# Moving the splitting of the turned x on VectorE, with other buffers for two x tiles and other steps for the weight splits, in a retention and feed-forward kernel

## The chip, the cores and the metric

The kernel runs on one core of one Trainium2 chip. The metric is the time of one execution on the device in microseconds (us), lower being better; the time of a kernel is the median of several runs. A profile is one execution taken by the hardware profiler: its span runs from the first instruction to the last. TensorE (matmul) is called PE in the profile, its weight loads PEld, VectorE is DVE, ScalarE is ACT, GpSimd is POOL and SyncE is SP; SP issues nearly all transfers of this kernel, in order.

## The reference

The input is `x`, four sequences of 1024 tokens with 512 features, in fp32. Two blocks follow each other, each wrapped by a layer norm before it, a layer norm after it and a residual addition.

```python
x = x + layernorm(attn(layernorm(x)))
x = x + layernorm(ffn(layernorm(x)))

def attn(x):                       # 16 heads of 32 features
    q, v = x @ Wq.T, x @ Wv.T
    ret = scan(v)                  # state = lam * state + v, along the tokens
    out = layernorm(q * ret) * gamma + beta
    return (out * silu(x @ Wg.T)) @ Wo.T

def ffn(x):                        # 512 -> 1536 -> 512, weights rounded to fp8
    gate = silu(x @ gate_w * gate_scale)
    return ((gate * (x @ up_w * up_scale)) @ down_w) * down_scale
```

## The kernel before

**Rounds and steps.** The 4096 tokens are worked on in eight blocks of 512 tokens (`TB`), each of four tiles of 128 tokens (`s` = 0 to 3). The features lie in four chunks of 128 (`c`). The main loop (`for t in range(NB)`, line 1221) has eight rounds; each has twelve steps `i`, one for each 128 of the 1536 inner features. In round `t` three blocks are in work. `f` is the feed-forward part of block `t`: in each step PE runs `f.gate(i)` (tile `pfg`), `f.up(i)` (`pfu`) and, two steps later, `f.down` (`pd`). `b` is the retention part of block `t + 1`, whose matmuls are put between those of the feed-forward part. `n` is block `t + 2`, whose x is loaded, normed and turned so that it can be used from step 11 on. `l` is the feed-forward part of the block before, which is finished in the first steps of the round.

**Order.** Every instruction of an engine runs in the order in which the program issues it (`InOrder`, line 66). So the position of a call in the long loop body is its place in the queues of all engines that it uses, and an instruction that waits holds back everything behind it on its engine. Buffers are tiles with a tag; a tag has a fixed number of slots that are handed out in turn, and a new tile waits until the last user of its slot is done.

**Three ways to project.** Blocks 0 and 1 use plain fp32 matmuls. Blocks 2 and 3 (`fast`) use a scheme with seven products of half size for each of the projections v, q and g. Blocks 4 to 7 (`by_parts`, `PARTS` = 4) use three passes for each chunk. For these the turned x and the weights are each split into a top part (a mask on the bits, `TOP_MASK`), the rest (`low`) and a combination (`diff`). `begin` runs the pass with the top part of the weights and the turned x, then the pass with `low`; `end` runs the pass with `diff`. The first `begin` (`v`, chunk 0) is issued in step 11 of the round before, right behind `f.up(11)` (`n.gap(-2)`). A pass multiplies by all 512 tokens, so it needs all four quarters of its operand. The output projection of every block from 2 on uses the seven products (`product`, tile `po`): in steps 7, 8 and 9, three, three and one of them. The first two are copied by ACT and the other five added by VectorE (`add_o`, tile `mids`); the order of the products is 1, 2, 6, 5, 3, 7, 4, and two PSUM banks are shared among them, so that a product which goes on in a bank waits until the addition of the one before has read it. Operands of the products are `y`, which VectorE finishes in step 6 (`gate_y`), and sums of its parts (`y_sums`).

**The turned x.** For block `t + 2`, in rounds 1 to 5, ACT norms x tile 0 in step 6, tiles 1 and 2 in step 7 and tile 3 in step 8 (`norm_x`, tile `xn`). VectorE turns each by blocks into a second tile, and SP sends it to DRAM (`send_x`, transfer `mx<-xn`). SP fetches it back in another layout (`fetch_x`, transfer `xnT<-mx`). For blocks 4 to 7, VectorE then makes for each quarter the mask and the rest (`low_of`: `top`, then `low`) and the combination (`diff_of`). For blocks 3 to 7 the normed and the turned tile are the halves of one pair, with a tag of a single slot (`xn`).

**The x1 tiles.** When the output products are added, `o_moments` takes means and variances on VectorE, POOL forms the power -1/2, ACT scales (`x1_of`) and POOL adds the residual x. `x1_moments` then takes the moments of this sum on VectorE, and `x1n_of` norms it. Tiles 0 and 1 go through this in steps 8 and 9, tiles 2 and 3 in steps 9, 10 and 11.

**The weight splits.** The weights of v, q and g are split for the three passes in twelve units (`Splitter`), during rounds 1 and 2. A unit is loaded by two transfers, split by three VectorE instructions and one POOL instruction (`split`, behind the step's `fuse`), and stored by two transfers at the end of the step (`store`). They are needed from the end of round 2 on. The condition `splits` says in which steps a unit is worked on.

## Time and profile before

| what | us |
|---|---|
| median of 3 runs (lowest, highest) | 985.81 (984.67, 986.65) |
| the profiled execution's own time | 983.96 |
| its span | 982.1 |
| PE busy | 952.0 (97%) |
| DVE busy | 682.5 (69%) |
| ACT busy | 427.5 (44%) |
| POOL busy | 279.5 (28%) |

The granted clock of TensorE is 0.995 of full speed over the span. The median of the runs lies 1.85 us above the profiled execution. Busy time is the time in which an engine executes an instruction; idle time before an instruction is put down to what released it. In the timelines below, a row holds the start, the duration, the engine, the instruction with its output and inputs, and in brackets the idle time before it with what ended it.

### The profile page before, as it was taken

The numbers are of one execution on the slowest core, as the hardware profiler recorded it, in microseconds if no ns is written. First come the engines' busy times: TensorE is split into PE (matmuls) and PEld (weight loads), VectorE is DVE, ScalarE is ACT, GpSimd is POOL, SyncE is SP. The second block draws the span as 40 slices with busy tenths as digits, with TensorE's granted clock in tenths as the row PEclk, the third lists the DMA queues.
The fourth block names the chain that finished last, engine by engine and source line by source line (L and its number), as shares of the span: only waits on it lengthen the run. The fifth ranks groups of instructions, "written<-read, shape, count | busy, mean of one in ns | idle before, by whom it ended". The sixth has DMA issues, their size and how long they took to land.

```text
span 982.1 us, 11944 instructions
## 1 busy us (share of the span) xinstructions
PE 952.0 (97%) x4022; PEld 746.3 (76%) x4022; DVE 682.5 (69%) x1054; ACT 427.5 (44%) x673; POOL 279.5 (28%) x340
## 2 busy tenths in 40 slices
PE   9999999999989999999999999999999999999996
PEld 7456766677868887778878788778878788788885
DVE  5996998768777877685476845867457765647445
ACT  3556674467645216332263424434263342624223
POOL 1405122403426134240242505322052322314020
PEclk9999999999999999999999999999999999999999
DMA  9311424766648556356454564555453564414021
GB/s 311 107 64 56 138 65 108 238 214 204 225 149 249 179 162 217 106 168 195 149 184 137 145 201 138 163 161 184 149 176 124 156 208 140 142 63 129 1 86 43
DMA packets 115500, 148.14 MB, mean 151 GB/s; under 512 B 10864, under 2 KB 60016, under 8 KB 115440
## 3 DMA queue, kind: packets, MB, share of 16 engines
q1 hardware_dynamic: 114576, 146.73, 47.7%
q8 instruction: 32, 0.52, 0.2%
q10 hardware_dynamic: 864, 0.66, 0.2%
q14 instruction: 28, 0.23, 0.1%
HBM read 108.02 MB, written 42.47 MB: 153 GB/s over the span
## 4 chain that ended last, share of the span: by engine, by line
PE 60%; DVE 17%; DMA 6%; ACT 6%; POOL 5%; issue 4%; SPq 1%; DVEq 0%; ACTq 0%; POOLq 0%
PE pfu L74 11%; PE pfg L74 10%; PE pd L74 9%; PE pv L74 9%; PE pq L74 8%; PE pg L74 6%; PE po L74 5%; DVE st L74 3%; DVE y L74 2%; DMA mx<-xn 1%; DVE gate L74 1%; SPq L74 1%; DVE mids L74 1%; DVE xs L74 1%; POOL mv L74 1%
## 5 line engine op out<-in xcount | busy, mean ns | idle before, releaser
L74 PE MATMUL pfu<-x1nT,up_sb 128*128 128x512 f32 x768 | 200.0, 402 | 1.8 <-DVE gate L74 1.8
L74 PE MATMUL pfg<-x1nT,gate_sb 128*128 128x512 f32 x768 | 194.8, 395 | 0.1
L74 PE MATMUL pd<-down_sb,fuse 128*128 128x512 f32 x720 | 184.1, 397 | 0.0
L74 PEld LDWEIGHTS pfu<-x1nT,up_sb 128*128 128x128 f32 x768 | 143.9, 188 | 36.2 <-DVE gate L74 3.9
L74 PEld LDWEIGHTS pfg<-x1nT,gate_sb 128*128 128x128 f32 x768 | 144.0, 188 | 30.4 <-DVE x1nT L74 0.9
L74 PEld LDWEIGHTS pd<-down_sb,fuse 128*128 128x128 f32 x720 | 135.5, 188 | 28.0
L74 ACT CAST fuse<-gate 128x512 fp32r<-128x512 f32 x90 | 55.7, 619 | 173.8 <-DVE gate L74 173.7
L74 DVE SCALAR_TENSOR_TENSOR gate<-pfu,us_sb,gate 128x512 f32<-128x512 f32 x96 | 71.7, 747 | 57.1 <-PE pfu L74 53.8
L74 ACT ACTIVATE gate<-pfg,gs_sb 128x512 f32<-128x512 f32 x96 | 65.6, 683 | 99.1 <-PE pfg L74 99.1
L74 POOL TENSOR_SCALAR mv<-mv 128x1 f32<-128x1 f32 (+1 forms) x82 | 24.7, 301 | 261.1 <-DVE mv L74 258.1
L74 DVE TENSOR_TENSOR fuse<-gate,fuse 128x512 fp32r<-128x512 f32 x90 | 76.6, 851 | 5.5 <-ACT fuse L74 5.5
L74 DVE BATCH_NORM_STATS2 st<-x 128x6 f32<-128x512 f32 x64 | 43.6, 681 | 20.7 <-POOL x L74 18.2
L74 POOL TENSOR_TENSOR ysum<-y 128x512 f32<-128x512 f32 (+1 forms) x10 | 12.0, 1201 | 148.2 <-DVE y L74 148.1
L74 POOL TENSOR_TENSOR mv<-mv,nhalf 128x1 f32<-128x1 f32 (+1 forms) x75 | 52.0, 694 | 6.2
L74 POOL TENSOR_TENSOR x<-x,x1n 128x512 f32<-128x512 f32 x32 | 45.7, 1432 | 10.0 <-ACT x1n L74 9.2
L74 POOL TENSOR_TENSOR d<-d,x 128x512 f32<-128x512 f32 x28 | 36.5, 1324 | 16.2 <-ACT d L74 10.8
L74 POOL TENSOR_TENSOR sqsum<-sqsum,sq 128x512 f32<-128x512 f32 x24 | 35.0, 1457 | 15.2 <-ACT sq L74 13.7
L74 POOL TENSOR_TENSOR ysum<-ysum,y 128x512 f32<-128x512 f32 (+1 forms) x20 | 24.1, 1203 | 53.5 <-DVE y L74 53.2
L74 DVE TENSOR_TENSOR y<-pq,y 128x512 f32<-128x512 f32 x18 | 12.4, 691 | 35.3 <-PE pq L74 35.3
L74 DVE RECIPROCAL rstd<-rstd 128x512 f32<-128x512 f32 x8 | 26.8, 3352 | 11.9 <-ACT rstd L74 11.9
L74 ACT ACTIVATE xn<-x,mv 128x512 f32<-128x512 f32 x28 | 22.2, 811 | 25.2 <-DMA mx<-xn 24.9
L74 PE MATMUL po<-w_ring_parts,t_sums 128*128 128x256 f32 x128 | 30.4, 380 | 2.3 <-issue 2.3
(199 smaller groups left out, 1616.4 us busy)
## 6 DMA issues: line engine op xcount, KB each, us to landing
kept<-x SPq DMA_DIRECT2D x32, 256.0 KB, 2.1
x<-kept SPq DMA_DIRECT2D x32, 256.0 KB, 4.4
x<-in_x SPq DMA_DIRECT2D x28, 256.0 KB, 3.9
w_ring_parts<-dsum_o SPq DMA_DIRECT2D x28, 256.0 KB, 2.7
out<-d SPq DMA_DIRECT2D x27, 256.0 KB, 2.0
mx<-xn SPq DMA_DIRECT2D x20, 256.0 KB, 2.0
xnT<-mx SPq DMA_DIRECT2D x64, 64.0 KB, 2.2
w_ring_parts<-dtop_v SPq DMA_DIRECT2D x16, 256.0 KB, 3.2
```

The costliest lines, as they stand in the source:

```text
L74: return lambda *args, **kwargs: tc.keep_in_program_order(op(*args, **kwargs))
```

## The change

Four things change, all for the later blocks.

- In `norm_x` and `send_x`, tiles 0 and 2 of blocks 3 to 7 take two slots of the tag `tok` (four slots, also used for the feed-forward outputs `d`, the `late` tiles and the normed x1 tiles) for the normed and the turned x. Tiles 1 and 3 keep the pair.
- `low_of(0)` moves from the end of step 7 into step 8, behind that step's first output product and ahead of `f.up(8)`. `low_of(1)` and `low_of(2)` move from the end of step 8 into step 9, behind the last output product and ahead of `x1_moments` of tiles 0 and 1.
- `low_of(3)` moves from ahead of `f.up(10)` to behind the `x1_moments` of tiles 2 and 3 in step 10; `x1n_of(2)` now stands ahead of `diff_of(3)`.
- The units of the weight splits are worked on in steps 1, 3, 4, 5, 8 and 9 of round 1 (before: 1 to 6, 8 and 9) and in steps 0 to 5 of round 2 (before: 0 to 3).

```diff
@@ norm_x
-            if self.t < 3:
+            if self.t < 3 or s % 2 == 0:
                 xn = work.tile([P, D], F32, tag="tok", name=f"xn_{self.t}_{s}", bufs=4)
@@ send_x
             if self.t < 3:
                 sq = work.tile([P, D], F32, tag="ret", name=f"xs_{self.t}_{s}")
+            elif s % 2 == 0:
+                sq = work.tile([P, D], F32, tag="tok", name=f"xs_{self.t}_{s}", bufs=4)
             else:
                 sq = self.pair[:, 1, :]
@@ main loop
-            splits = (t == 1 and 1 <= i < 10 and i != 7) or (t == 2 and i < 4)
+            splits = (t == 1 and i in (1, 3, 4, 5, 8, 9)) or (t == 2 and i < 6)
...
             if fast and 7 <= i < 10:
                 b.product()
+            if n and n.by_parts and i in (8, 9):
+                for s in ([0], [1, 2])[i - 8]:
+                    n.low_of(s)
...
-            if n and n.by_parts and i == 10:
-                n.low_of(3)
             if fast and i == 10:
                 b.x1_of(2)
                 b.x1_of(3)
...
             if fast and i == 10:
                 b.x1_moments(2)
                 b.x1_moments(3)
                 if n and n.by_parts:
+                    n.low_of(3)
+                b.x1n_of(2)
+                if n and n.by_parts:
                     n.diff_of(3)
-                b.x1n_of(2)
...
-            if n and n.by_parts and i in (7, 8):
-                for s in ([0], [1, 2])[i - 7]:
-                    n.low_of(s)
```

## The prediction

> **What bounds the kernel now.** I read the page's busy shares, then TensorE's waits, then its timeline, and last the timelines of the engines that it waits for.

> ```profile
> PE 952.0 (97%) x4022; PEld 746.3 (76%) x4022; DVE 682.5 (69%) x1054; ACT 427.5 (44%) x673; POOL 279.5 (28%) x340
> ```

> TensorE is busy for 97% of the span. None of its work changes, so only its gaps, 30 us in all, can move. The waits say where they lie (total, times, longest):

> ```profile
> PE po L74 <- issue: 9.3, 4, 3.6
> PE pfu L74 <- DVE gate L74: 1.8, 5, 0.6
> PE po L74 <- DVE mids L74: 1.7, 3, 0.7
> ```

> The largest gaps stand at the output products (`po`, steps 7 to 9 of a round) and at step 11's `pfu`. Below I write `t/i` for round t, step i, and count from the start of step 7's `pfg` in its round: 273.21 (t=1), 398.59, 518.00, 633.17, 748.83 and 865.25 (t=6). Round 6 prepares no later x and has no gap there: it gives the undisturbed clock. In it `po` 1 starts at 1.81, `pfu` 7 at 3.35, the seventh product at 23.13 and the next `pfu` at 24.67. The others take 30.21, 30.24, 25.99, 26.46 and 27.18 us from `pfg` 7 to that `pfu`: 5.54, 5.57, 1.32, 1.79 and 2.51 lost in t=1 to 5. TensorE's timeline (start, duration, instructions, idle time before them and what ended it) has the two large gaps, the seventh product to the low pass in t=3, and the seventh product of t=6:

> ```profile
> 278.80 3.65 PE L74 MATMUL po<-w_ring,y 128*128 128x256 f32 x8 [3.62 <-issue]
> ...
> 418.35 3.51 PE L74 MATMUL po<-w_ring,t_sums 128*128 128x256 f32 x8 [3.38 <-issue]
> ...
> 542.34 1.99 PE L74 MATMUL po<-w_ring_parts,y 128*128 128x256 f32 x8 [0.73 <-DVE mids L74]
> ...
> 555.54 2.11 PE L74 MATMUL pfu<-x1nT,up_sb 128*128 128x512 f32 x8 [0.31 <-DVE gate L74]
> ...
> 558.43 1.07 PE L74 MATMUL pv<-low,w_ring_parts 128*128 128x512 f32 x4
> 559.34 1.99 PE L74 MATMUL pd<-down_sb,fuse 128*128 128x512 f32 x8
> ...
> 888.38 1.89 PE L74 MATMUL po<-w_ring_parts,y 128*128 128x256 f32 x8
> ```

> After a gap of 3.4 us eight `po` matmuls take 3.5 to 3.65 us; undisturbed they take 1.89. The table by stretches names the cause (stretch, length, busy time of PE, PEld, DVE, ACT and POOL, then the granted clock, DMA share and GB/s):

> ```profile
> 275.20:278.80 3.60, 0.00 (x1) 0.03 (x1) 3.53 (x7) 2.52 (x3) 1.32 (x3) 0.98 0.27 80
> 278.80:282.10 3.30, 3.30 (x9) 2.35 (x9) 3.23 (x4) 0.95 (x3) 2.07 (x2) 0.50 0.00 0
> ...
> 766.50:768.10 1.60, 1.59 (x8) 1.42 (x9) 0.57 (x1) 1.00 (x2) 0.00 (x0) 1.00 1.01 338
> ```

> It is 0.50 after 3.6 us of idleness, and still 1.00 after the 1.49 us gap of t=5.

> VectorE's timeline in t=3 shows what the change touches:

> ```profile
> 526.93 0.43 DVE L74 TENSOR_SCALAR top<-xnT 128x512 int32<-128x512 int32 x1 [2.55 <-DMA xnT<-mx]
> ...
> 531.68 0.71 DVE L74 STREAM_TRANSPOSE xn<-xn 128x512 f32<-128x512 f32 x1 [2.97 <-ACT xn L74]
> ...
> 544.38 0.69 DVE L74 TENSOR_TENSOR mids<-po,mids 128x512 f32<-128x512 f32 x1 [1.01 <-PE po L74]
> ...
> 554.74 0.74 DVE L74 SCALAR_TENSOR_TENSOR gate<-pfu,us_sb,gate 128x512 f32<-128x512 f32 x1
> 556.00 0.69 DVE L74 BATCH_NORM_STATS2 st<-x 128x6 f32<-128x512 f32 x1 [0.52 <-POOL x L74]
> ...
> 557.36 0.69 DVE L74 BATCH_NORM_STATS2 st<-x 128x6 f32<-128x512 f32 x1 [0.44 <-POOL x L74]
> ```

> Early in the stage VectorE stands still, with the products' additions queued behind it (526.93, 531.68); over all rounds its waits and ACT's say:

> ```profile
> DVE top L74 <- DMA xnT<-mx: 14.9, 4, 5.1
> ...
> ACT xn L74 <- DMA mx<-xn: 24.9, 5, 7.2
> ```

>  From the seventh product's addition (544.38) on it has almost no pause, and the next gaps of TensorE wait for it.

> **The change, part by part.**

> *Token buffers (t=1 to 5).* `norm_x(2)` no longer waits until `send_x(1)`'s transfer has left the pair; ACT waits there 24.9 us in five rounds, and VectorE's transposition waits for ACT (2.97 above). Nothing is added. The token slots are used 12 times a round instead of 8. The slot of `d` is stored by 500.9 in t=3 and taken at 517.9, and `late`'s stores in t=2 are issued by 394.0 and the slot taken at 400.0, so I cost the extra turns at 0. Without that cover the price is one store, 2.0 us from issue to landing.

> *`low_of(0)` from 7 to 8, behind the fourth product.* It is 0.43 and 0.69 us of work; its wait for the transfer (14.9 us in four rounds) goes, since the data arrive 8.9 to 12.4 us after `pfg` 7 and it now comes at about 15.1. With both waits gone VectorE adds products 3, 4 and 6 when TensorE ends them (10.9, 14.4, 21.5); the next uses of those banks are at 19.6, 16.0 and 23.1. So steps 7 to 9 run as in round 6 and the 1.32, 1.79 and 2.51 us come back in t=3 to 5. No DMA is moved on SP except the two sends, which come earlier.

> *`low_of(1)`, `low_of(2)` and `low_of(3)`: where it is paid.* The first two take 2.13 us (539.47 to 541.60). They lay ahead of the sixth product's addition; they now come after the seventh's, which cannot start before 25.06 (round 6: 890.31). All that follows on VectorE moves back by 2.13: moments, `diff_of`, `x1n_of`, and the moments of output tiles 2 and 3. From the latter a chain through POOL's power, ACT's scaling and POOL's addition leads to the moments of x1: 4.51 us from 551.49 to 556.00 and 6.76 to the end of the second (558.25); round 6 gives 4.36 and 6.73 with less on VectorE, so this chain is latency and does not shrink. `low_of(3)`, formerly ahead of `fuse` 10, now waits for its end, and the low pass of step 11 waits for `low_of(3)`, needing all four quarters. Counted from the seventh addition: second moments end at 13.87 (558.25 - 544.38) + 2.13 = 16.00, `low_of(3)` at 17.14, low pass at about 17.2, with 0.1 for restarting. It was at 14.05 (558.43 - 544.38). So the low pass starts at 25.06 + 17.2 = 42.27, the `pd` behind it at 43.28. On the way `pfu` 11 waits about 1.5 us for `fuse` 10, and the low pass some 1.9; undisturbed they would start at 35.75 and 38.51. That `pd` now starts at 41.34, 41.82 and 42.56 in t=3 to 5. Cost: 1.94 + 1.46 + 0.72 = **+4.12**, gains of the previous paragraph included. Behind it, `x1n_of(2)`, `diff_of(3)`, `fuse` 11 and `x1n_of(3)` keep their distance from `pd` within 0.1.

> The price of `low_of` beside POOL is not shown there. Bounds: 0.43 + 0.69 alone, or, from the split instructions beside POOL's sums (358.00 to 360.60), 1.10 for the second, 0.8 us more a round. I take the low value: by the distances above POOL's additions end at 25.5 and the first mask starts at 25.7. The other bound, below, is VectorE's work without the POOL latency: 0.52 + 1.07 + 0.44 = 2.0 us less a round. That ACT/POOL chain is equal in round 6, so I don't take it.

> *Splits.* One is 1.78 us of VectorE (265.01 to 266.79) and 1.05 of POOL, with two loads and two stores on SP. In 1/6 it stood ahead of `gate_y(0)` and `gate_y(1)`, whose results product 1 needs. Without it `gate_y(0)` ends at 3.70 after `pfg` 7 and `gate_y(1)` at 4.40; the six matmuls that need the second take 1.16, so `pfu` 7 starts at 5.65 instead of 8.89: **-3.24**, half of it clock. In 1/2, the split delayed the addition at 236.04, which waits for a product ended by 234.8, and with it POOL's row sum and `mu` (waits of 0.20 and 0.65): about 1.0 of the step's 11.41 us, between 0.5 and 1.3: **-1.0**. In 2/4 it costs nothing: 1/4 has it and takes the same 11.21 us as 2/4 without. In 2/5 it puts t=2 where t=1 is without 1/6: `pfu` 7 is 2.3 late. Its `pd` after the low pass then starts at 43.28 + 2.3 = 45.58, and was at 45.59: **0**. On SP the issues of a split (0.3 to 0.6 us each) go ahead of the loads of x in 2/4, issued by 385.4 and first used at 393.0, and of the last weights for step 7, issued at 395.1; on POOL its 1.05 goes ahead of the additions of `d` and of a power that 2/6 needs at 397.0. The slack of 5 us and more covers them; without it each would cost its own 2 us.

> Sum: -3.24 - 1.0 + 0 + 4.12 = **-0.1 us**. The profiled execution took 983.96 (its span 982.1 and 1.9 around it), 1.85 below the median of the runs, 985.81; against the median the forecast is 985.7.

> [...] The trace: 3.38 us of idleness brought the clock down, 1.49 did not. [...] A DVE `TENSOR_SCALAR` of x1n takes 0.54 alone (319.02) and 1.50 beside POOL's `t_sums` (320.29). [...]

> **The rivals.** *Slower, by the clock.* The gaps at the low pass (1.9 after 1.5, with 2.9 us of work between) and at product 1 in t=1 and 2 (1.8 and 0.7) may also halve the clock. At 418.35 the halved clock cost 1.75 us beyond the gap (product and `pd` took 5.31 to 423.66, undisturbed 3.56), at 278.80 1.2 (six matmuls took 2.3, not 1.16). Six places of about 1.5 give up to +9, two of them already +3: 989 to 995. It decides from the second place. For it: gaps crowd in steps 10 and 11. Against: 1.49 at 766.51 and 1.16 plus 0.46 at 195 to 196 left 1.00.

> *Faster, by a shorter moments chain.* If the x1 moments in step 10 did not wait for POOL, each of four low passes would come up to 2.0 earlier: -2 to -8, 978 to 984. The equal 4.36 to 4.51 in all rounds speaks against it.

> *The masks' waits stay.* If the sends or turned x still arrive late, t=3 to 5 keep their losses and pay 3.2 a round in addition: about +5, 991. Data arriving 3 us before use in the slowest round speak against it.

> **How the numbers follow.** My forecast, within a few steps' errors of nothing (1.7 us): 0.58, of which 0.46 is within 0.2% (2 us, about what a measurement here can tell from no change), 0.06 faster, 0.06 slower. Clock 0.20, shorter chain 0.14, waits that stay 0.08. So faster 0.20, same 0.46, slower 0.34. The range leaves out the far halves of the faster and slower cases: 982 to 991.

> **What would show it.** Right: no gap above 0.3 us at `po` 3 to 7; `DVE top <- DMA` and `ACT xn <- DMA` gone; a new wait of the `pv` low pass for VectorE's `low`, near 1.9 us in four rounds; `pfu` 11 waiting 1.5; `po` 1 waiting 1.8 in t=1 and t=2; clock 1.00 throughout. Wrong: low passes at 40 after `pfg` 7, or PEclk of 0.5 in step 11.

## The result, and the profile after

| | before | after |
|---|---|---|
| median, us | 985.3 | 992.39 |
| lowest and highest of six runs | 984.34, 987.34 | 989.44, 995.48 |
| profiled execution, its span | 983.96, 982.1 | 991.58, 989.8 |
| mean granted clock in it | 0.995 | 0.992 |

The runs of this table were made beside each other. The ratio after to before is 1.007, with a 95% interval of 1.0048 to 1.0091: the change makes the kernel slower, by 0.7%. The forecast was "no change", 985.7, and its range ended at 991; it was wrong, and the rival "Slower, by the clock" (989 to 995) came true.

The busy shares hardly move. PE's 2.3 us more are the first hint, since it executes the same 4022 matmuls:

```profile
PE 954.3 (96%) x4022; PEld 748.0 (76%) x4022; DVE 679.1 (69%) x1054; ACT 427.3 (43%) x673; POOL 273.0 (28%) x340
```

TensorE's waits after (total, times, longest) have changed places. The gaps of the products by `issue` fell from 9.3 to 3.7 us in all and are at most 1.8 long. The wait of the low pass for VectorE's `low` is new, 8.6 us in four rounds, and `pfu` 11 waits three times as long as before:

```profile
PE pv L74 <- DVE low L74: 8.6, 4, 2.4
PE pfu L74 <- DVE gate L74: 5.5, 5, 1.3
PE po L74 <- issue: 3.7, 2, 1.8
```

TensorE's timeline of after, with the second product of t=1 and t=2, step 11 of t=3, and the low passes of t=4 and t=5:

```profile
276.56 3.11 PE L74 MATMUL po<-w_ring,y 128*128 128x256 f32 x8 [1.82 <-issue]
...
400.22 3.54 PE L74 MATMUL po<-w_ring,y 128*128 128x256 f32 x8 [1.83 <-issue]
...
554.79 2.11 PE L74 MATMUL pfu<-x1nT,up_sb 128*128 128x512 f32 x8 [1.27 <-DVE gate L74]
...
559.91 1.20 PE L74 MATMUL pv<-low,w_ring_parts 128*128 128x512 f32 x4 [2.06 <-DVE low L74]
560.94 3.58 PE L74 MATMUL pd<-down_sb,fuse 128*128 128x512 f32 x8
...
678.78 1.19 PE L74 MATMUL pv<-low,w_ring_parts 128*128 128x512 f32 x4 [2.06 <-DVE low L74]
679.82 1.99 PE L74 MATMUL pd<-down_sb,fuse 128*128 128x512 f32 x8
...
796.40 2.03 PE L74 MATMUL pv<-low,w_ring_parts 128*128 128x512 f32 x4 [2.41 <-DVE low L74]
```

The gaps are where the prediction put them, and nearly as long. But look at the durations behind them. Eight matmuls of `pd` take 3.58 us in t=3 and 1.99 in t=4, after the same gap of 2.06. The table by stretches (stretch, length, busy time of PE, PEld, DVE, ACT and POOL, granted clock, DMA share, GB/s) says why, for the product of t=2 and for the `pd` of t=3 and of t=4:

```profile
400.20:403.60 3.40, 3.38 (x9) 2.50 (x10) 3.33 (x4) 1.20 (x2) 1.98 (x2) 0.55 0.00 0
560.90:564.30 3.40, 3.40 (x9) 2.49 (x9) 3.03 (x6) 2.14 (x4) 0.00 (x0) 0.51 0.32 82
679.80:681.60 1.80, 1.80 (x9) 1.45 (x8) 1.71 (x3) 1.59 (x4) 0.00 (x0) 1.00 0.12 25
```

Gaps of 1.83 and of 2.06 us were followed by a clock of one half; another of 2.06 was not. The 0.55 and 0.51 are means of these stretches, which begin a little before the fall: the clock itself stood at 0.50 for 3.41 us, from 400.54 and from 560.97 on. In what they differ is shown in the last section.

### The profile page after: what moved, and what is told of

It is laid out like the page before. It is cut to its first block, busy times and chain, and to the rows that moved or that the text cites. A ratio compares the mean times of both kernels' runs of the same rounds, so it can differ in the third digit from the quotient of the medians.

```text
span 989.8 us, 11929 instructions
## 1 busy us (share of the span) xinstructions
PE 954.3 (96%) x4022; PEld 748.0 (76%) x4022; DVE 679.1 (69%) x1054; ACT 427.3 (43%) x673; POOL 273.0 (28%) x340
## 4 chain that ended last, share of the span: by engine, by line
PE 38%; DVE 8%; POOL 4%; ACT 3%; issue 3%; DMA 1%; SPq 0%; DVEq 0%; POOLq 0%; ACTq 0%
PE pd L74 8%; PE pfg L74 8%; PE pfu L74 8%; PE pv L74 4%; PE po L74 4%; PE pq L74 3%; PE pg L74 2%; DVE st L74 2%; DMA kept<-x 1%; POOL x L74 1%; POOL d L74 1%; ACT x1n L74 1%; DVE diff L74 1%; DVE low L74 1%; POOL mvd L74 1%
## 5 line engine op out<-in xcount | busy, mean ns | idle before, releaser
L74 PE MATMUL pfu<-x1nT,up_sb 128*128 128x512 f32 x768 | 201.6, 405 | 5.5 <-DVE gate L74 5.5
L74 PE MATMUL pfg<-x1nT,gate_sb 128*128 128x512 f32 x768 | 194.7, 395 | 0.1
L74 PE MATMUL pd<-down_sb,fuse 128*128 128x512 f32 x720 | 186.0, 400 | 0.0
L74 PEld LDWEIGHTS pfu<-x1nT,up_sb 128*128 128x128 f32 x768 | 144.6, 189 | 41.0 <-DVE gate L74 8.6
L74 PEld LDWEIGHTS pfg<-x1nT,gate_sb 128*128 128x128 f32 x768 | 144.0, 188 | 30.4 <-DVE x1nT L74 0.8
L74 PEld LDWEIGHTS pd<-down_sb,fuse 128*128 128x128 f32 x720 | 136.8, 190 | 28.5
L74 ACT CAST fuse<-gate 128x512 fp32r<-128x512 f32 x90 | 55.6, 618 | 183.5 <-DVE gate L74 183.5
L74 DVE SCALAR_TENSOR_TENSOR gate<-pfu,us_sb,gate 128x512 f32<-128x512 f32 x96 | 71.8, 748 | 59.6 <-PE pfu L74 53.6
L74 ACT ACTIVATE gate<-pfg,gs_sb 128x512 f32<-128x512 f32 x96 | 65.6, 684 | 105.4 <-PE pfg L74 105.3
L74 POOL TENSOR_SCALAR mv<-mv 128x1 f32<-128x1 f32 (+1 forms) x82 | 23.8, 290 | 253.0 <-DVE mv L74 249.9
L74 DVE TENSOR_TENSOR fuse<-gate,fuse 128x512 fp32r<-128x512 f32 x90 | 73.9, 821 | 5.5 <-ACT fuse L74 5.5
L74 DVE BATCH_NORM_STATS2 st<-x 128x6 f32<-128x512 f32 x64 | 43.6, 681 | 25.3 <-POOL x L74 22.6
L74 POOL TENSOR_TENSOR ysum<-y 128x512 f32<-128x512 f32 (+1 forms) x10 | 12.0, 1202 | 156.8 <-DVE y L74 156.7
L74 POOL TENSOR_TENSOR mv<-mv,nhalf 128x1 f32<-128x1 f32 (+1 forms) x75 | 50.9, 679 | 6.2
L74 DVE TENSOR_TENSOR mids<-po,mids 128x512 f32<-128x512 f32 x30 | 20.5, 684 | 36.4 <-PE po L74 36.3
L74 POOL TENSOR_TENSOR x<-x,x1n 128x512 f32<-128x512 f32 x32 | 41.5, 1298 | 12.7 <-ACT x1n L74 12.0
L74 POOL TENSOR_TENSOR d<-d,x 128x512 f32<-128x512 f32 x28 | 36.2, 1317 | 16.1 <-ACT d L74 14.1
L74 POOL TENSOR_TENSOR sqsum<-sqsum,sq 128x512 f32<-128x512 f32 x24 | 35.1, 1464 | 14.9 <-ACT sq L74 13.5
L74 POOL TENSOR_TENSOR ysum<-ysum,y 128x512 f32<-128x512 f32 (+1 forms) x20 | 23.1, 1157 | 54.3 <-DVE y L74 54.0
L74 DVE TENSOR_TENSOR y<-pq,y 128x512 f32<-128x512 f32 x18 | 12.4, 691 | 35.7 <-PE pq L74 35.7
L74 POOL TENSOR_SCALAR split_room<-split_room 128x512 f32<-128x512 f32 x12 | 9.5, 788 | 93.2 <-DVE split_room L74 93.2
L74 DVE RECIPROCAL rstd<-rstd 128x512 f32<-128x512 f32 x8 | 26.8, 3352 | 11.8 <-ACT rstd L74 11.8
```

The lines of the kernel that those rows point to most:

```text
L74: return lambda *args, **kwargs: tc.keep_in_program_order(op(*args, **kwargs))
```

## The experiments

**Theory and rivals.** Theory: VectorE's chain went as forecast, and the clock, halved behind the new gaps, is the missing time. First rival: the clock is a small part, and the chain itself is later than forecast. Second rival: the split steps cost more than worked out. The parts were then tried one by one, to find which of them makes the gaps.

**Filling the gaps: `e1_filled` and `e9_half_filled`.** Against after:

```diff
+            again = 3 if (k, c, part) == ("v", 0, "top") else 1
-            for i in range(NC):
+            for i in list(range(NC)) * again:
...
-            project(pg, gate_sb, i, self.parts)
+            for _ in range(2 if self.t in (1, 2) and i == 7 else 1):
+                project(pg, gate_sb, i, self.parts)
```

The first `top` pass of step 11 is made three times, and the `pfg` of step 7 twice in t=1 and 2; nothing on the other engines changes. `e9_half_filled` makes only that `top` pass twice.

> The changed kernel with its two kinds of new gaps filled by repeated TensorE work: in step 11 the top pass of v, chunk 0, of blocks 4 to 7 is issued three times (each time starting the sum anew, 1.9 us more work in a gap of 2.05 to 2.4), and in step 7 of rounds 1 and 2 the gate projection is issued twice (1.8 us more in a gap of 1.8). Clock theory: the gaps lie in the waits, so the added 11 us of matmuls cost almost nothing, no row behind them is at half clock, the granted clock is 0.995 or more, the time falls by about 4 to 5 us from 992.4 to 987 to 988.5 and the runs lie within 2 us of each other. Rival (the rows behind a wait are slow for another reason, such as transfers or VectorE's traffic at that moment): the slow rows stay, the repeated work delays what follows, 992 to 996, and the runs scatter by 6 us as before.

> The changed kernel with only one repetition of the top pass in step 11 (gap at the low pass 2.05 to 1.1) and nothing added in step 7. If the clock falls when idle time within some 3.4 us passes a threshold, shorter gaps let it fall in fewer rounds at the low pass, while the two first products of rounds 1 and 2 may still lose 0.7 to 1.1 each: 988 to 990. If any gap near 1 us beside that of 1.28 brings it down: 992. If the low pass is not what costs: 992.

`e1_filled` took 987.32 us (ratio to before 1.0021, 1.0012 to 1.003), so more work on TensorE made after 5 us faster. Its timeline in step 11 of t=3:

```profile
557.96 1.19 PE L74 MATMUL pv<-low,w_ring_parts 128*128 128x512 f32 x4 [0.15 <-DVE low L74]
558.99 2.00 PE L74 MATMUL pd<-down_sb,fuse 128*128 128x512 f32 x8
```

That `pd` starts 43.43 us after the round's `pfg` 7, within 0.01 us of its place in after (43.44): VectorE's chain is untouched. Only its duration is another, 2.00 and not 3.58. The round's end (the next round's first `pfg`, counted from `pfg` 7) gives the price of the clock round by round:

| | t=1 | t=2 | t=3 | t=4 | t=5 |
|---|---|---|---|---|---|
| before | 52.39 | 51.06 | 46.81 | 47.28 | 48.03 |
| after | 50.63 | 52.71 | 50.51 | 48.90 | 50.85 |
| `e1_filled` | 49.10 | 51.19 | 48.92 | 48.89 | 49.28 |
| after less `e1_filled` | 1.53 | 1.52 | 1.59 | 0.01 | 1.57 |

The four differences stand in the four rounds in which a halved clock was granted, and t=4, where it was not, has none: 6.2 us in all. `e9_half_filled`, 987.22 us (1.0015, 1.0003 to 1.0028), a little below the 988 to 990 expected, leaves about half the gap at the low pass, 1.10 in t=2 to 4 and 1.46 in t=5, still behind a gap of 1.27; the clock fell behind none of them. It did fall at the second product of t=1, unfilled there (`pfu` 7 at 6.39 and not 5.63), and not at that of t=2, unfilled too. So the clock theory is shown.

**The parts: `e8_tokens_only`, `e3_splits_only`, `e4_no_splits`.** The first is before with the token buffers alone (the edits of `norm_x` and `send_x`), the second before with the new `splits` condition alone, the third after with the old condition, hence buffers and masks.

```diff
 e8_tokens_only, against before
-            if self.t < 3:
+            if self.t < 3 or s % 2 == 0:
...
+            elif s % 2 == 0:
+                sq = work.tile([P, D], F32, tag="tok", name=f"xs_{self.t}_{s}", bufs=4)
 e3_splits_only, against before
-            splits = (t == 1 and 1 <= i < 10 and i != 7) or (t == 2 and i < 4)
+            splits = (t == 1 and i in (1, 3, 4, 5, 8, 9)) or (t == 2 and i < 6)
 e4_no_splits, against after
-            splits = (t == 1 and i in (1, 3, 4, 5, 8, 9)) or (t == 2 and i < 6)
+            splits = (t == 1 and 1 <= i < 10 and i != 7) or (t == 2 and i < 4)
```

> The kernel before with one edit: in t=3 to 5 the x tiles 0 and 2 are normed in token buffers; masks and splits stay as before. This separates the buffers from the masks. If the buffers alone free ACT and VectorE, ACT's waits of xn for the transfer of mx (24.9 us over five rounds) and VectorE's wait for the turned x (14.9 over four) shrink, the 7th product's pfu 9 comes at 24.7 after pfg 7 in t=3 to 5 instead of 25.99, 26.46 and 27.18, and the pd after the low pass at 40.0 to 41 instead of 41.34, 41.82 and 42.56: 3 to 4 us off, 980 to 983 us. If the gaps at the products come from where low_of(0) stands (step 7, ahead of the third product's addition, waiting for its transfer), the buffers alone leave them, pfu 9 stays within 0.3 of before, and the time is 984 to 986.

> The kernel before with only the new steps of the weight splits. By the terms of the prediction round 1 gains 4.2 (3.2 at the first output product, 1.0 at mu), less what the clock takes; the changed kernel's profile showed 2.1 there. Round 2 loses 2.3 at its first product; its later gap of 3.4 us, which waits for transfers, may take part of that up. Sum between -3 and +1.5: 982 to 987. Rival, that the splits are the part that makes the changed kernel slower: 990 or more.

> The changed kernel with the splits in the steps of before: masks and buffers alone. Round 1 as in the kernel before (first product 5.5 late). Round 2: without the split in step 5 the pd behind the low pass starts at 43.4 instead of 45.6, gain 2.2 or more. Rounds 3 to 5: losses of 2.1, 1.6 and 0.9 at full clock. Sum +2.4 at full clock, 987.7; each halving of the clock at one of the four low passes adds 1.6, so 988 to 994, scattering from run to run. Rival, that the masks cost nothing by themselves: 983 to 985.

| | median, us | ratio to before, interval |
|---|---|---|
| `e8_tokens_only` | 979.6 | 0.9944 (0.9927 to 0.996) |
| `e3_splits_only` | 982.96 | 0.998 (0.9968 to 0.9991) |
| `e4_no_splits` | 993.29 | 1.0088 (1.0073 to 1.0103) |

Two of the three parts are gains; `e3_splits_only` and `e4_no_splits` took the time expected. The buffers take ACT's waits away and with them nearly all of the 3.38 us gap of t=2 (0.30 is left) and the lateness peculiar to t=4 and 5: the `pd` behind the low pass starts at 41.55, 41.35, 41.34 and 41.34 in t=2 to 5. The expectation that product 7 would then start undisturbed was a miss; it waits 1.05 to 1.06 us, since the masks of quarters 1 and 2 still lie ahead of the sixth addition:

```profile
539.31 1.99 PE L74 MATMUL po<-w_ring_parts,y 128*128 128x256 f32 x8 [1.06 <-DVE mids L74]
```

VectorE's long wait for the turned x (14.8 us over four rounds) remains in this run, so it cost the products nothing by itself.

`e4_no_splits` differs from `e8_tokens_only` in the masks' places alone, and takes 13.7 us more. By rounds, t=2 to 5 end 2.01, 3.67, 3.69 and 4.07 later, 13.4 in all: some 2.0 to 2.5 each by the later low pass, and about 1.6 in three of them by the clock. The masks are what makes after slower. The second rival falls.

In `e3_splits_only` the product behind the gap of t=2 has a row that I had not expected. The gap is as long as before's, 3.38, yet the matmuls take 1.97 us where before they took 3.51:

```profile
417.67 1.97 PE L74 MATMUL po<-w_ring,t_sums 128*128 128x256 f32 x8 [3.38 <-issue]
```

**Which masks: `e2_low3_back`, `e5_low12_ahead`, `e6_masks_in_pauses`.** All against after. The first puts `low_of(3)` back ahead of `f.up(10)`, as in before, and `diff_of(3)` ahead of `x1n_of(2)`; the second moves `low_of(1)` and `low_of(2)` ahead of the seventh product's addition, into the pause that VectorE has there; the third does that and has `low_of(3)` ahead of the moments of x1.

```diff
 e2_low3_back
+            if n and n.by_parts and i == 10:
+                n.low_of(3)
...
-                    n.low_of(3)
-                b.x1n_of(2)
-                if n and n.by_parts:
                     n.diff_of(3)
+                b.x1n_of(2)
 e5_low12_ahead, and in e6_masks_in_pauses too
+            if n and n.by_parts and i == 9:
+                n.low_of(1)
+                n.low_of(2)
...
-                for s in ([0], [1, 2])[i - 8]:
-                    n.low_of(s)
+            if n and n.by_parts and i == 8:
+                n.low_of(0)
 e6_masks_in_pauses
-                b.x1_moments(2)
-                b.x1_moments(3)
                 if n and n.by_parts:
                     n.low_of(3)
+                b.x1_moments(2)
+                b.x1_moments(3)
```

> The changed kernel with low_of(3) ahead of the up projection of step 10, and diff_of(3) ahead of x1n_of(2), as in the kernel before. By the chain of the prediction (14.05 + 2.13 from the seventh addition) the low pass then starts 41.3 us after step 7 begins in rounds 3 to 5, without a wait of its own, the pd behind it at 42.3 instead of 43.4; pfu 11 waits 2.5 to 2.7 us in one piece instead of 1.28. So 4 times 1.1 less: 988, if the clock falls as often as in the changed kernel; if single gaps of 2.6 us bring it down in every round, 991 to 993. Rival, that the order around low_of(3) doesn't matter because VectorE is simply full: 992.

> The changed kernel with low_of(1) and low_of(2) in step 9 ahead of the seventh output product, where VectorE waits 2.26 us for TensorE in the changed kernel; low_of(3) stays behind the x1 moments. By the chain the moments and low_of(3) come 2.13 earlier: low pass at 40.3 to 40.5 from the start of step 7 instead of 42.4, pfu 11 without a wait (35.8), so one gap of about 1.8 us a round at the low pass, in rounds 2 to 5. At full clock 4 times 2.1 less than the changed kernel with full clock (987.3 with filled gaps, less 0.6), 978 to 980; with the clock falling in some rounds 979 to 983. Rival, that the wait for the low pass comes from low_of(3)'s place alone and the first two masks are harmless: 988 to 992.

> As the one before, and low_of(3) directly behind fuse 10, ahead of the x1 moments, where VectorE waits 1.47 us for POOL's addition in the changed kernel. All three masks then stand in pauses: no wait at pfu 11 nor at the low pass, pd behind it at 39.4 to 39.8 in rounds 3 to 5 and 41.7 to 42.1 in round 2. Sum against the kernel before from its profile's places: -1.9, -2.4, -3.1 in rounds 3 to 5, -3.5 to -3.9 in round 2, -3 to -4 in round 1: 985.3 - 14 to 15, so 970 to 972.5 us. Rival, that TensorE's clock or transfers take part of this back: 974 or more.

`e2_low3_back` took 983.21 us (0.9974, 0.9963 to 0.9986), faster than expected. The low pass waits for nothing, `pfu` 11 waits 2.34 us in one piece, and the `pd` starts at 42.16 to 42.19 in t=3 to 5. The clock fell behind that gap in t=2 and not in t=3, 4 and 5 (here t=2 and t=3):

```profile
436.81 3.36 PE L74 MATMUL pfu<-x1nT,up_sb 128*128 128x512 f32 x8 [2.34 <-DVE gate L74]
...
554.41 2.14 PE L74 MATMUL pfu<-x1nT,up_sb 128*128 128x512 f32 x8 [2.34 <-DVE gate L74]
```

`e5_low12_ahead` is the largest miss: 990.59 us (1.0048, 1.0031 to 1.0064), where 979 to 983 was expected and 988 to 992 by its rival. The four instructions would have fitted into the pause at their old durations. Beside POOL's two additions of x they take 4.26 us and not 2.13, and the seventh addition (last row) starts 1.8 us late. VectorE's timeline in t=3:

```profile
539.00 0.42 DVE L74 TENSOR_SCALAR top<-xnT 128x512 int32<-128x512 int32 x1
539.46 1.64 DVE L74 TENSOR_TENSOR low<-xnT,top 128x512 fp32r<-128x512 f32 x1
541.02 1.51 DVE L74 TENSOR_SCALAR top<-xnT 128x512 int32<-128x512 int32 x1
542.57 0.69 DVE L74 TENSOR_TENSOR low<-xnT,top 128x512 fp32r<-128x512 f32 x1
543.18 0.68 DVE L74 TENSOR_TENSOR mids<-po,mids 128x512 f32<-128x512 f32 x1
```

and POOL's beside it:

```profile
539.15 3.10 POOL L74 TENSOR_TENSOR x<-x,x1n 128x512 f32<-128x512 f32 x2 [0.33 <-ACT x1n L74]
```

The `pd` comes only 0.3 us earlier than in after (43.12), with both gaps still there.

`e6_masks_in_pauses` took 977.99 us (0.9918, 0.9896 to 0.9939) against an expected 970 to 972.5. The greater part of the miss goes with the same stretching of masks (VectorE is busy for 690.2 us, against 679.1 in after, with the same 1054 instructions): the `pd` comes 1.0 to 1.4 us a round later than expected, in four rounds. About 1.2 more is the clock, which fell at the second product of t=1 (`pfu` 7 at 6.79 and not 5.63). Its low pass has no gap, `pfu` 11 waits 1.07, the `pd` stands at 40.78 to 40.82 in t=3 to 5. Compared with `e5_low12_ahead`, the place of `low_of(3)` alone is worth 2.3 us a round, and it dissolves the second gap and the clock's fall with it. So `low_of(3)` behind the moments of x1 is the costly move.

**Versions that beat both: `e7_pauses_splits`, `e10_tokens_splits`, `e11_masks_spread`.** All have a third list of split steps, which keeps the units away from step 6 of t=1 and step 5 of t=2:

```diff
+            splits = (t == 1 and i in (1, 2, 3, 4, 7, 8, 9)) or (t == 2 and i < 5)
 e11_masks_spread, places of the masks (low_of(3) as in before)
+            if n and n.by_parts and i in (8, 9):
+                n.low_of(0 if i == 8 else 2)
...
+            if n and n.by_parts and i == 8:
+                n.low_of(1)
```

`e7_pauses_splits` is `e6_masks_in_pauses` with it, `e10_tokens_splits` is `e8_tokens_only` with it. `e11_masks_spread` is the latter with quarter 0 behind the fourth product, quarter 1 at the end of step 8 and quarter 2 behind the seventh product.

> As the one before, with the split of step 5 taken out of rounds 1 and 2 (steps 1 to 4 and 7 to 9 of round 1, 0 to 4 of round 2), so that gate_y is not held up ahead of the first output product. First product without its wait of 1.83 in both rounds: pfu 7 at 3.4 instead of 5.63, -2.2 each; the split back in step 2 of round 1 costs up to 0.8. Sum 966 to 969. Rival, that a split in step 7 of round 1 holds up the additions of products 3 and 4 as much: 970 or more.

> The kernel before with the token buffers and a list of split steps of its own (1 to 4 and 7 to 9 of t=1, 0 to 4 of t=2, so neither step 6 of t=1 nor step 5 of t=2); the masks stay as before. If the buffers and the splits act apart, as the sum of the two would have it, this is the 979.6 of the buffers alone less what the splits bring in t=1: pfu 7 at 3.5 after pfg 7 and not 8.93, some 5.4 us, so 974 to 975. If the splits moved into steps 7 to 9 of t=1 run into the sends and the product additions there, the gain stays under 3 us and the time is 977 or more.

> As the run of buffers and splits, but with the masks spread: quarter 0 in step 8 behind the fourth product, quarter 1 at the end of step 8, quarter 2 in step 9 behind the seventh product, quarter 3 as before behind fuse 10. Contention with POOL's x additions and the length of the work behind the seventh addition are the two prices of a mask. If both are as the earlier runs show, product 7 no longer waits 1.05 us in t=3 to 5 (pfu 9 at 24.7), one mask instead of none lies behind the seventh addition, and the pd after the low pass stands at 40.2 to 40.9 instead of 41.34: 0.5 to 1.1 us a round for four rounds, 970 to 973 us. If quarter 1's mask alone still delays the sixth addition, pfu 9 stays near 26 and the time is 975 or more.

| | median, us | ratio to before, interval | `pd` in t=3 to 5 |
|---|---|---|---|
| `e7_pauses_splits` | 972.71 | 0.9866 (0.9849 to 0.9882) | 40.78 to 40.81 |
| `e10_tokens_splits` | 973.25 | 0.9885 (0.9868 to 0.9901) | 41.34 to 41.36 |
| `e11_masks_spread` | 974.04 | 0.9886 (0.9871 to 0.9902) | 41.34 to 41.35 |

The three can't be told apart. In all of them `pfu` 7 starts at 3.48 to 3.49 in t=1 and 2, without a gap at the second product, and the mean clock of the profiled executions is 0.999, 0.999 and 0.996 (in the last it fell once, at 228.12 in t=1, behind a wait of 1.98 for weights). `e10_tokens_splits` came within 0.8 us of its expectation of 974 to 975: buffers and splits act apart, and masks left where they were are the simplest way to 12 us. `e7_pauses_splits` missed its 966 to 969 as the run before it did. `e11_masks_spread` shows why moving masks brings so little: product 7 no longer waits (`pfu` 9 at 24.92), but `pfu` 11 waits 1.38 us instead of 0.30, and the `pd` is where it was. The expected 0.5 to 1.1 us a round did not come.

## Why the prediction was wrong

**Right: the chain.** Forecast for t=3 to 5 were the low pass at 42.27 and its `pd` at 43.28; they came at 42.39 to 42.75 and, in t=3 and 4, at 43.44 and 43.43. The waits were 1.27 at `pfu` 11 (1.5 forecast), 2.06 at the low pass (1.9) and 1.82 at the second product of t=1 and 2 (1.8). The gaps at products 3 to 7 vanished, as did the two waits for transfers. That the masks go at their short durations was right as well: in t=3 the first starts at 543.17, 0.05 us after POOL's second addition has ended, and the four take 0.42, 0.69, 0.42 and 0.69. Two masks that began while POOL's additions of x ran (539.15 to 542.25 in `e5_low12_ahead`) took longer: 1.64 for `low` at 539.46 and 1.51 for `top` at 541.02. Nine that such an addition joined later were not stretched: `top` at 539.00 in the same run took 0.42, and before has eight, two in each of t=2 to 5, all at 0.69 (in t=3 `low` at 541.00, POOL's addition starting at 541.02, and `low` at 554.13, the addition starting at 554.56). So in these rows the order of the two starts parts the long masks from the short ones.

**Wrong: "clock 1.00 throughout", and the sum's gaps of 1.9 us at no price.** No run shows that gaps of 1.9 us come at no price: after 1.83 and 2.06 the clock was 0.50 at some places and 1.00 at others. The prediction's rows had 1.00 after 1.49 us and one half after 3.38 and 3.6, with nothing between, and that 1.9 would go with the first was its author's estimate. The clock was halved at four of the six places that the rival named, at 1.52 to 1.59 us each (about 1.5 there): 6.2 of the 7.8 us between the forecast of -0.1 and the +7.7 of the two spans. The row that misled was the gap of 1.49 at 766.51: it shows that 1.49 was free there, and nothing of 1.8 or 2.06. Of the gaps of 2.06 the one in t=3 was charged and the one in t=4 was not, which goes with where each lies on a grid of 3.41 us (last section), and the prediction had no term for that.

**Terms that were mis-sized.** The rest is about 1.6 us: without the clock the sum comes to +1.5 and not -0.1, from the rounds of `e1_filled` and, for steps 0 to 6, of after:

| term | forecast | measured without the clock |
|---|---|---|
| first product of t=1 | -3.24 | -3.29 (52.39 to 49.10) |
| steps 2 and 3 of t=1 | -1.0 | -0.35 |
| round 2 | 0 | +0.17 |
| t=3 to 5 | +4.12 | +4.97 (2.11, 1.61, 1.25) |

The second row is three things: step 3 of t=1 became 1.63 us shorter, more than forecast; steps 4 to 6 took 0.86 back, mostly by a new wait of `pg` for ACT's `mids` (0.64); and steps 0 to 2 were 0.42 longer by a transfer of weights (`w_ring<-dsum_q`) that came later. In the last row t=3 and t=4 are about 0.16 over each. In t=5 it is 0.5: the low pass waits 2.41, because the last mask there first waits 0.40 us for the transfer `kept<-x` (795.19), which the other rounds' don't.

**The other rivals.** Data arriving late, and a shorter chain of moments, both fell: `DVE top <- DMA` is gone, and the chain has the forecast length.

**What was mis-judged beyond the sum.** The forecast treated buffers, masks and splits as one trade. By themselves the buffers bring 0.56% and the splits 0.2%; the masks' move costs 1.4% (13.7 us) on top of the buffers, and for it the products gain only the 1.3 us a round that the buffers had left (`pfu` 9 at 24.67 and not 26.00 in t=3).

## What to carry to other kernels

## What the runs showed of the hardware that was not expected

- **Gaps of 1.8 to 2.4 us were followed by a halved clock at some places and not at others, and a grid in time parts them.** Places of one kind, counted over the profiled executions of after and of the experiments in which they occur (a fall is read from the durations behind the gap and from the granted clock):

| gap | falls / places | in |
|---|---|---|
| 1.8, second product of t=1 and 2 | 4 / 12 | after, `e2_low3_back`, `e3_splits_only`, `e5_low12_ahead`, `e6_masks_in_pauses`, `e9_half_filled` |
| 1.0 to 1.3, and 2.0 to 2.4 some 3 us later, step 11 | 8 / 12 | after, `e4_no_splits`, `e5_low12_ahead` |
| 1.27, and 1.1 to 1.5 some 3 us later, step 11 | 0 / 4 | `e9_half_filled` |
| 2.34 alone, step 11 | 1 / 4 | `e2_low3_back` |
| 3.38 at a product of t=2 | 1 / 2 | before, `e3_splits_only` |

  Two shares of this table, 8/12 for the four low passes and 4/12 for the two products, would make the clock's part of after 3.3 x 1.55 = 5.2 us on the mean, an estimate. The traces show the falls on a grid in time. A fall lasted 3.41 us (one, in `e8_tokens_only`, twice that), and the falls of one execution started whole multiples of 3.413 us apart: in after at 277.66, 400.54, 560.97 and 796.49, which is 36, 47 and 69 steps, in before at 278.65 and 418.60, which is 41. Stretches of after cut at these steps (stretch, length, busy time of PE, granted clock, DMA share, GB/s), for the gaps of 2.06 in t=3 and in t=4:

```profile
557.55:560.97 3.42, 1.36 (x7) 1.00 0.72 239
560.97:564.38 3.41, 3.41 (x10) 0.50 0.32 82
...
677.02:680.43 3.41, 1.65 (x7) 1.00 0.58 182
680.43:683.85 3.42, 3.42 (x21) 1.00 0.23 77
```

  In t=3 the whole gap lies in one stretch, and TensorE idles 2.06 us of it. In t=4 the step at 677.02 cuts 0.30 us off the same gap; 1.76 is left, and the clock stays. All 13 profiled executions were cut in this way (some 3600 stretches, without the first 10 us and what lies behind 965): each of the 19 falls from full clock stands right behind a stretch in which TensorE idled 1.82 us or more, and in no other stretch did it idle longer than 1.82. The two nearest are after's at 274.25, with a fall behind it, and that of `e5_low12_ahead` at 395.79, with none; the times are not sharp enough to part these two, so in these executions the falls begin at some 1.8 us. Behind 965, after has one stretch that does not fit, at 980.81: TensorE idled 1.85 us of it, and the clock behind it was 1.00. The 0 of 4 of `e9_half_filled` goes with the rest, since neither gap reaches 1.8 and 4.0 us of work lie between them; and the gap of 3.38 in `e3_splits_only`, which no fall followed, was cut by a step into 1.71 and 1.67. The grids of before and after lie apart (the falls at 278.65 and at 277.66 by 0.99 us, no multiple of the step), so in another execution an equal gap can be cut at another place.
- **The scatter of after's runs goes with that clock.** Its six times with their mean granted clocks are 989.44 (0.994), 991.58 (0.992), 991.77 (0.991), 993.01 (0.991), 993.45 (0.989) and 995.48 (0.988): 0.006 of clock on 990 us is 5.9 us, and the times span 6.0. So after has no one time, and the range of a forecast for it should hold the spread.
